# A three-layer CIN kernel on one core: set-up reordered, two weight rows made inside the loop, issue order fixed on all engines

## The chip, the cores and the metric

The kernel runs on one core of one Trainium2 chip. The metric is the device time of one execution in microseconds (us), the median over several executions. All times below are microseconds unless another unit is written. The span of a profile is from the first to the last instruction. The execution profiled before the change took 556.77 (span 555.0), more than the median of 552.89.

The engines are TensorE (PE, with its weight loads as PEld), VectorE (DVE), ScalarE (ACT), GpSimd (POOL) and SyncE (SP), which only starts DMAs here. TensorE has a granted clock, recorded in the profile: 1.00 is full speed, 0.50 is half.

## The reference

The input is x of shape (1024, 64, 16): batch, fields, embedding. Three layers multiply fields pairwise and contract the products with a weight:

```python
def _cin_forward(x, Ws, bs, fc_w, fc_b, split_half=True):
    x0 = x
    h = x
    xs = []
    n = len(Ws)                       # 3 layers of 128 channels
    for i in range(n):
        z = jnp.einsum('bfe,bge->bfge', x0, h)
        ...
        y = jnp.einsum('oc,bce->boe', Ws[i], z) + bs[i][None, :, None]
        if split_half and i != n - 1:
            half = y.shape[1] // 2
            x_i, h = (y[:, :half, :], y[:, half:, :])
        else:
            x_i, h = (y, y)
        xs.append(x_i)
    pooled = jnp.sum(jnp.concatenate(xs, axis=1), axis=2)
    return pooled @ fc_w.T + fc_b
```

The result is one number per batch row, and everything behind the second product is linear. Both kernels therefore fold `fc_w` into the weights first (set-up: a vector V2 from W2, a matrix M from V2 and W1, rows V1 and V0 from the other halves of W1 and W0), and then need, per chunk of 32 batch rows, only the pairwise products of x and one contraction of 17 matmuls.

## The kernel before

There are 32 chunks. Each has four products `z` made by VectorE (2.29 each), each of which feeds four matmuls, then a matmul of squares. Every second chunk closes a pair: TensorE makes one more matmul, `y`, VectorE multiplies it into `uu` and reduces. These are the parts that matter:

```python
    xp = ctx.enter_context(tc.tile_pool(name="xp", bufs=3))
    zp = ctx.enter_context(tc.tile_pool(name="zp", bufs=3))
    ...
    pv2 = ps.tile([128, 32], F32, tag="set", name="pv2", bufs=4)      # V2: 32 matmuls of one column
    for k in range(32):
        nc.tensor.matmul(pv2[:, k : k + 1], w2s[:, k, :], fc2, start=True, stop=True)
    ...
    for k in range(4):                                                # V1 and V0, in set-up
        w01 = setup.tile([128, 1024], F32, tag="w01", name=f"w01_{k}")
        nc.sync.dma_start(out=w01, in_=wv01[:, k * 1024 : (k + 1) * 1024])
        for m in range(2):
            pv = ps.tile([2, 512], F32, tag="set", name=f"pv_{k}_{m}", bufs=4)
            nc.tensor.matmul(pv, fc01, w01[:, m * 512 : (m + 1) * 512], start=True, stop=True)
            ...
    def products(c, j):
        z = zp.tile([128, NI, N], F32, tag="z", name="z")
        nc.vector.tensor_tensor(
            z, xas[c], xbs[c][:, j, :].unsqueeze(1).to_broadcast([128, NI, N]), ALU.mult
        )
        for i in range(NI):
            t = j * NI + i
            nc.tensor.matmul(accs[c], w_all[:, t, :], z[:, i, :], start=(t == 0), stop=False)
    ...
    def combine(c):
        ...
        nc.scalar.copy(q, accs[c][64:128])
        nc.vector.scalar_tensor_tensor(uu[to, 0, :], accs[c][0:64], bh1, q, ALU.add, ALU.mult)
        if half == 0:
            return
        y = ps.tile([128, N], F32, tag="y", name=f"y_{c}", bufs=1)
        nc.tensor.matmul(y, bd, xxs[c // 2], start=True, stop=True)
        nc.vector.scalar_tensor_tensor(uu[:, 1, :], y, cx, xxs[c // 2], ALU.add, ALU.mult)
        nc.vector.tensor_reduce(
            acc[:, :, c // 2, :], uu.rearrange("p k (b e) -> p k b e", e=E), AX.X, ALU.add
        )

    for c in range(NCH + 1):
        if c + 1 < NCH:
            load_chunk(c + 1)
        if c < NCH:
            accs[c] = ps.tile([128, N], F32, tag="acc", name=f"acc_{c}")
            products(c, 0)
            products(c, 1)
        if c > 0:
            combine(c - 1)
        if c < NCH:
            products(c, 2)
            products(c, 3)
            squares(c)
```

The text puts `combine` in the middle of a chunk, but before the change this text was not the issue order: the scheduler of the language was free to put instructions that don't depend on one another in another order on each engine, and did.

Of the kernel before, what the change touches and what calls it, by code (L numbers as in the profile page):

```python
# [26 lines left out]
F32 = mybir.dt.float32  # L27
AF = mybir.ActivationFunctionType
ALU = mybir.AluOpType
AX = mybir.AxisListType  # L30

F = 64
# [12 lines left out]
def cin_kernel(ctx, tc, x2, w0a, w0b, w1h, wv2, wv01, b0, b1, b2, fc_w, fc_b, out):  # L45
    nc = tc.nc
    const = ctx.enter_context(tc.tile_pool(name="const", bufs=1))
    setup = ctx.enter_context(tc.tile_pool(name="setup", bufs=2))
    xp = ctx.enter_context(tc.tile_pool(name="xp", bufs=3))
    zp = ctx.enter_context(tc.tile_pool(name="zp", bufs=3))  # L50
    sp = ctx.enter_context(tc.tile_pool(name="sp", bufs=2))
    ps = ctx.enter_context(tc.tile_pool(name="ps", bufs=2, space=bass.MemoryType.PSUM))
# [9 lines left out]


    fc01 = const.tile([128, 2], F32, tag="fc01", name="fc01")
    fc2 = const.tile([128, 1], F32, tag="fc2", name="fc2")
    nc.gpsimd.memset(fc01, 0.0)
    nc.scalar.dma_start(out=fc2, in_=fc_w[0, 128:256].unsqueeze(1))
    nc.scalar.dma_start(out=fc01[0:64, 0:1], in_=fc_w[0, 0:64].unsqueeze(1))
    nc.scalar.dma_start(out=fc01[64:128, 1:2], in_=fc_w[0, 64:128].unsqueeze(1))
    bh1 = const.tile([F, 1], F32, tag="bh1", name="bh1")  # L70
# [6 lines left out]
    nc.gpsimd.dma_start(out=bh1, in_=b0c[64:128])  # L77
# [20 lines left out]


    w2s = const.tile([128, 32, 128], F32, tag="w2s", name="w2s")  # L100
    w1s = const.tile([128, 32 * F], F32, tag="w1s", name="w1s")
    w0t = const.tile([128, NT + 1, F], F32, tag="w0t", name="w0t")
    w0u = const.tile([128, NT, F], F32, tag="w0u", name="w0u")
    for k in range(4):
        nc.sync.dma_start(out=w2s[:, 8 * k : 8 * k + 8, :], in_=wv2[:, 8 * k : 8 * k + 8, :])
    nc.sync.dma_start(out=w1s, in_=w1h)

    xas, xbs, zls, xxs = {}, {}, {}, {}

    def load_chunk(c):  # L110
        xa = xp.tile([128, NI, N], F32, tag="xa", name=f"xa_{c}")
        xb = xp.tile([128, NJ, N], F32, tag="xb", name=f"xb_{c}")
        zl = xp.tile([128, N], F32, tag="zl", name=f"zl_{c}")
        for half in range(2):
            to = slice(half * F, (half + 1) * F)
            nc.sync.dma_start(out=xa[to], in_=rows(c, 0, [[1, NI]]))
            nc.sync.dma_start(out=xb[to], in_=rows(c, 16 * half + 4, [[4, NJ]]))
        nc.sync.dma_start(out=zl[F:128], in_=rows(c, 0, []))
        if c % 2 == 0:
            xxs[c // 2] = sp.tile([128, N], F32, tag="xx", name=f"xx_{c}")  # L120
        to = slice(c % 2 * F, (c % 2 + 1) * F)
        nc.sync.dma_start(out=xxs[c // 2][to], in_=rows(c, 0, []))
        xas[c], xbs[c], zls[c] = xa, xb, zl

    load_chunk(0)
# [5 lines left out]
    pv2 = ps.tile([128, 32], F32, tag="set", name="pv2", bufs=4)  # L131
    for k in range(32):
        nc.tensor.matmul(pv2[:, k : k + 1], w2s[:, k, :], fc2, start=True, stop=True)  # L133
    for half in range(2):
        to = slice(half * F, (half + 1) * F)
        nc.vector.tensor_copy(v2t[to, 0:32], pv2[0:64])  # L136
        nc.vector.tensor_copy(v2t[to, 32:64], pv2[64:128])  # L137
# [3 lines left out]
    m_sb = const.tile([F, F, F], F32, tag="m_sb", name="m_sb")  # L141
    for m in range(4):
        for half in range(2):
            to = slice(half * F, (half + 1) * F)
            pm = ps.tile([F, 512], F32, tag="set", name=f"pm_{m}_{half}", bufs=4)
            nc.tensor.matmul(  # L146
                pm, v2t[to], w1s[to, m * 512 : (m + 1) * 512], start=True, stop=True
            )
            f0 = half * 32 + m * 8
            m_to = m_sb[:, f0 : f0 + 8, :].rearrange("p f g -> p (f g)")  # L150
            if half:
                nc.vector.tensor_copy(m_to, pm)  # L152
            else:
                nc.scalar.copy(m_to, pm)
    md = dr.tile([EXT, EXT, F], F32, tag="md", name="md")
    nc.scalar.dma_start(out=md[0:64, 0:64, :], in_=m_sb)
    nc.scalar.dma_start(out=md[64:96, 0:64, :], in_=m_sb[0:32])
    nc.scalar.dma_start(out=md[0:64, 64:96, :], in_=m_sb[:, 0:32, :])
    nc.scalar.dma_start(out=md[64:96, 64:68, :], in_=m_sb[0:32, 0:4, :])
    nc.scalar.dma_start(out=md[64:68, 64:96, :], in_=m_sb[0:4, 0:32, :])  # L160
# [9 lines left out]
    for half in range(2):  # L170
        to = slice(half * F, (half + 1) * F)
        b = 16 * half + 4
        nc.scalar.dma_start(
            out=ms1[to].rearrange("p (j i) g -> p j (i g)", i=NI),
            in_=skewed(b * row, [[4 * row, NJ], [1, NI * F]]),
        )
        for i in range(NI):
            nc.scalar.dma_start(
                out=ms2[to].rearrange("p (j i) g -> p j i g", i=NI)[:, :, i, :],
                in_=skewed(i * row + b * F, [[4 * F, NJ], [1, F]]),  # L180
            )
    nc.scalar.dma_start(out=w_all[0:64, NT, 64:128], in_=skewed(0, [[1, F]]))

    nc.vector.memset(ms2[64:128, 3 * NI, :], 0.0)  # L184
    nc.vector.memset(w0u[64:128, 3 * NI, :], 0.0)
    nc.vector.tensor_tensor(w_all[:, 0:NT, 0:64], w0t[:, 0:NT, :], w0u, ALU.add)
    nc.vector.tensor_copy(w_all[0:64, NT, 0:64], w0t[0:64, NT, :])
    nc.vector.tensor_tensor(w_all[:, 0:NT, 64:128], ms1, ms2, ALU.add)  # L188


    vrow = const.tile([2, F * F], F32, tag="vrow", name="vrow")
    for k in range(4):
        w01 = setup.tile([128, 1024], F32, tag="w01", name=f"w01_{k}")
        nc.sync.dma_start(out=w01, in_=wv01[:, k * 1024 : (k + 1) * 1024])
        for m in range(2):
            pv = ps.tile([2, 512], F32, tag="set", name=f"pv_{k}_{m}", bufs=4)
            nc.tensor.matmul(pv, fc01, w01[:, m * 512 : (m + 1) * 512], start=True, stop=True)  # L197
            col = (2 * k + m) * 512
            nc.scalar.copy(vrow[:, col : col + 512], pv)  # L199
    nc.scalar.dma_start(  # L200
        out=w_all[64:128, NT, 64:128], in_=vrow[1:2, :].rearrange("o (f g) -> o f g", g=F)
    )
    for half in range(2):
        to = slice(half * F, (half + 1) * F)
        nc.scalar.dma_start(
            out=bd[to, to], in_=vrow[0:1, :].rearrange("o (f g) -> o f g", g=F)
        )


    cx = const.tile([128, 1], F32, tag="cx", name="cx")  # L210
    pcx = ps.tile([128, 1], F32, tag="set", name="pcx", bufs=4)
    for half in range(2):
        nc.tensor.matmul(
            pcx[half * F : (half + 1) * F], v2t[0:64], bh2, start=True, stop=True
        )
    nc.scalar.copy(cx, pcx)
    cst = const.tile([1, 1], F32, tag="cst", name="cst")
    pc = ps.tile([1, 1], F32, tag="set", name="pc", bufs=4)
    for j in range(2):
        nc.tensor.matmul(  # L220
            pc, fcol[:, j : j + 1], bcol[:, j : j + 1], start=(j == 0), stop=(j == 1)
        )
    nc.scalar.activation(cst, pc, AF.Identity, bias=fcb, scale=float(E))
# [5 lines left out]
    def products(c, j):  # L229
        z = zp.tile([128, NI, N], F32, tag="z", name="z")  # L230
        nc.vector.tensor_tensor(  # L231
            z, xas[c], xbs[c][:, j, :].unsqueeze(1).to_broadcast([128, NI, N]), ALU.mult
        )
        for i in range(NI):
            t = j * NI + i
            nc.tensor.matmul(accs[c], w_all[:, t, :], z[:, i, :], start=(t == 0), stop=False)  # L236

    def squares(c):
        nc.scalar.activation(zls[c][0:64], xas[c][0:64, 0, :], AF.Square)  # L239
        nc.tensor.matmul(accs[c], w_all[:, NT, :], zls[c], start=False, stop=True)  # L240

    def combine(c):
        half = c % 2
        to = slice(half * F, (half + 1) * F)
        if half == 0:
            uus[c // 2] = sp.tile([128, 2, N], F32, tag="uu", name=f"uu_{c}")
        uu = uus[c // 2]
        q = sp.tile([F, N], F32, tag="q", name=f"q_{c}")
        nc.scalar.copy(q, accs[c][64:128])  # L249
        nc.vector.scalar_tensor_tensor(uu[to, 0, :], accs[c][0:64], bh1, q, ALU.add, ALU.mult)  # L250
        if half == 0:
            return
        y = ps.tile([128, N], F32, tag="y", name=f"y_{c}", bufs=1)
        nc.tensor.matmul(y, bd, xxs[c // 2], start=True, stop=True)  # L254
        nc.vector.scalar_tensor_tensor(uu[:, 1, :], y, cx, xxs[c // 2], ALU.add, ALU.mult)  # L255
        nc.vector.tensor_reduce(  # L256
            acc[:, :, c // 2, :], uu.rearrange("p k (b e) -> p k b e", e=E), AX.X, ALU.add
        )

    for c in range(NCH + 1):  # L260
        if c + 1 < NCH:
            load_chunk(c + 1)
        if c < NCH:
            accs[c] = ps.tile([128, N], F32, tag="acc", name=f"acc_{c}")
            products(c, 0)
            products(c, 1)
        if c > 0:
            combine(c - 1)
# [7 lines left out]
    for k in range(2):  # L276
        po = ps.tile([1, 2, half_pairs * CB], F32, tag="set", name=f"po_{k}", bufs=4)
# [63 lines left out]
```

## Time and profile before

| | before |
|---|---|
| median of 3 runs | 552.89 (551.77 to 554.76) |
| profiled span, mean granted clock | 555.0, 0.975 |
| first product matmul | 66.3 |
| TensorE busy, share of the span | 515.9, 93% |
| one pair of chunks in the loop | 30.04 |

Most lines that show this are in the prediction below. Two more matter. They are groups of the page: line, engine, operation, output and inputs with their sizes and the count; then busy time and the mean ns of one; then the engine's idle time just before them and what ended most of it.

```profile
L236 PE MATMUL acc<-z,w_all 128*128 128x512 f32 x1024 | 447.2, 592 | 0.0
L231 DVE TENSOR_TENSOR z<-xa,xb 128x2048 f32<-128x2048 f32 x128 | 293.3, 2292 | 135.9 <-PE acc L236 134.6
```

TensorE never idles in front of a product pass (0.0). VectorE idles 135.9 in front of its products, and 134.6 of that ends when TensorE frees a buffer. VectorE is ahead, and TensorE sets the pace.

### The profile page before, as it was taken

How to read it: one execution, taken by the hardware profiler on the slowest of the kernel's cores; microseconds unless marked ns; L12 is line 12 of the kernel's file. 1: busy time of each engine (PE TensorE's matmuls, PEld its weight loads, DVE VectorE, ACT ScalarE, POOL GpSimd, SP SyncE). 2: the span in 40 equal slices, each digit the busy share in tenths (PEclk: the TensorE clock that was granted, in tenths of full speed). 3: DMA queues.
4: the chain of work that ended last, by engine and by line, in shares of the span. 5: the costliest groups of instructions: out<-in, count | busy, mean ns of one | idle time of the engine just before them, and what ended most of it. 6: DMA issues, size and time to landing. Idle time of an engine off the chain costs nothing.

```text
span 555.0 us, 3402 instructions
## 1 busy us (share of the span) xinstructions
PE 515.9 (93%) x1240; PEld 231.9 (42%) x1240; DVE 352.0 (63%) x205; ACT 44.9 (8%) x81; POOL 5.3 (1%) x18
## 2 busy tenths in 40 slices
PE   5803799999999999999999999999999999999997
PEld 5600144444444444444444444444444444444442
DVE  0250076768677677768676867767776867686751
ACT  0100300000000000000000000000000000000001
POOL 3000000000000000000000000000000000000000
PEclk9967699999999999999999999999999999999999
DMA  8999998787777777877778777777787877874000
GB/s 254 185 283 210 205 208 170 144 163 146 156 153 159 150 152 162 180 161 161 160 147 165 146 154 154 154 150 154 161 180 161 165 155 151 162 152 77 0 1 0
DMA packets 33114, 85.33 MB, mean 154 GB/s; under 512 B 6405, under 2 KB 6949, under 8 KB 28710
## 3 DMA queue, kind: packets, MB, share of 16 engines
q1 hardware_dynamic: 29234, 81.84, 71.1%
q10 hardware_dynamic: 3608, 3.28, 2.8%
q8 instruction: 10, 0.16, 0.2%
q14 instruction: 6, 0.05, 0.0%
q0 software_dynamic: 256, 0.00, 0.0%
HBM read 82.89 MB, written 2.17 MB: 153 GB/s over the span
## 4 chain that ended last, share of the span: by engine, by line
PE 92%; DMA 6%; DVE 0%; ACT 0%; issue 0%; ACTq 0%; SPq 0%
PE acc L236 79%; PE acc L240 5%; DMA w<-in_wv 3%; PE pv L133 2%; PE y L254 2%; PE pv L197 2%; DMA ms<-md 1%; DMA fc<-in_fc_w 1%; DMA md<-m_sb 1%; PE pm L146 1%; PE po L281 0%; DVE acc L256 0%; DVE uu L255 0%; ACT res L289 0%; ACT q L249 0%
## 5 line engine op out<-in xcount | busy, mean ns | idle before, releaser
L236 PE MATMUL acc<-z,w_all 128*128 128x512 f32 x1024 | 447.2, 592 | 0.0
L231 DVE TENSOR_TENSOR z<-xa,xb 128x2048 f32<-128x2048 f32 x128 | 293.3, 2292 | 135.9 <-PE acc L236 134.6
L236 PEld LDWEIGHTS acc<-z,w_all 128*128 128x128 f32 x1024 | 194.5, 190 | 244.5 <-issue 244.4
L249 ACT COPY q<-acc 64x512 f32<-64x512 f32 x32 | 18.6, 582 | 443.8 <-PE acc L240 443.8
L197 PE MATMUL pv<-w,fc 128*2 128x512 f32 x16 | 11.5, 887 | 27.9 <-DMA w<-in_wv 14.9
L240 PE MATMUL acc<-zl,w_all 128*128 128x512 f32 x64 | 32.7, 592 | 0.0
L250 DVE SCALAR_TENSOR_TENSOR uu<-acc,bh,q 64x512 f32<-64x512 f32 x32 | 23.7, 740 | 10.0 <-ACT q L249 9.5
L239 ACT ACTIVATE zl<-xa 64x512 f32<-64x512 f32 x32 | 20.1, 628 | 3.6 <-DMA xa<-in_x 3.6
L133 PE MATMUL pv<-fc,w2s 128*128 128x1 f32 x64 | 13.8, 352 | 6.6 <-DMA fc<-in_fc_w 6.6
L256 DVE TENSOR_REDUCE acc<-uu 128x64 f32<-128x1024 f32 x16 | 19.5, 1220 | 0.5
L240 PEld LDWEIGHTS acc<-zl,w_all 128*128 128x128 f32 x64 | 12.2, 190 | 15.3 <-issue 15.3
L197 PEld LDWEIGHTS pv<-w,fc 128*2 128x2 f32 x16 | 1.6, 108 | 37.6 <-issue 21.5
L133 PEld LDWEIGHTS pv<-fc,w2s 128*128 128x128 f32 x64 | 13.7, 332 | 6.6 <-DMA fc<-in_fc_w 6.6
L254 PE MATMUL y<-xx,bd 128*128 128x512 f32 x32 | 16.3, 592 | 0.0
L136 DVE COPY v2t<-pv 64x32 f32<-64x32 f32 x2 | 0.4, 184 | 20.4 <-PE pv L133 20.4
L255 DVE SCALAR_TENSOR_TENSOR uu<-y,cx,xx 128x512 f32<-128x512 f32 x16 | 11.9, 745 | 0.0
L188 DVE TENSOR_TENSOR w_all<-ms,ms 128x1024 f32<-128x1024 f32 x1 | 1.2, 1224 | 13.2 <-DMA ms<-md 13.2
L254 PEld LDWEIGHTS y<-xx,bd 128*128 128x128 f32 x32 | 6.1, 190 | 7.7 <-issue 7.7
L199 ACT COPY vrow<-pv 2x512 f32<-2x512 f32 x8 | 4.2, 570 | 33.3 <-DMA ms<-md 32.2
L184 DVE MEMSET ms<- 64x64 f32 x1 | 0.1, 112 | 9.7 <-DMA ms<-md 9.7
L146 PE MATMUL pm<-w1s,v2t 64*64 64x512 f32 x16 | 5.6, 809 | 0.5 <-DVE v2t L137 0.5
L152 DVE COPY m_sb<-pm 64x512 f32<-64x512 f32 x4 | 2.7, 683 | 3.2 <-PE pm L146 3.2
(33 smaller groups left out, 21.0 us busy)
## 6 DMA issues: line engine op xcount, KB each, us to landing
xa<-in_x SPq DMA_DIRECT2D x64, 512.0 KB, 5.8
xb<-in_x SPq DMA_DIRECT2D x64, 512.0 KB, 7.1
zl<-in_x SPq DMA_DIRECT2D x32, 128.0 KB, 4.2
xx<-in_x SPq DMA_DIRECT2D x32, 128.0 KB, 4.1
w2s<-in_wv SPq DMA_DIRECT2D x4, 512.0 KB, 7.8
w<-in_wv SPq DMA_DIRECT2D x4, 512.0 KB, 11.9
w1s<-in_w1h SPq DMA_DIRECT2D x1, 1024.0 KB, 13.4
md<-m_sb ACTq DMA_DIRECT2D x2, 512.0 KB, 7.1
```

The costliest lines, as they stand in the source:

```text
L133: nc.tensor.matmul(pv2[:, k : k + 1], w2s[:, k, :], fc2, start=True, stop=True)
L146: nc.tensor.matmul(pm, v2t[to], w1s[to, m * 512 : (m + 1) * 512], start=True, stop=True)
L197: nc.tensor.matmul(pv, fc01, w01[:, m * 512 : (m + 1) * 512], start=True, stop=True)
L231: nc.vector.tensor_tensor(z, xas[c], xbs[c][:, j, :].unsqueeze(1).to_broadcast([128, NI, N]), ALU.mult)
L236: nc.tensor.matmul(accs[c], w_all[:, t, :], z[:, i, :], start=(t == 0), stop=False)
L239: nc.scalar.activation(zls[c][0:64], xas[c][0:64, 0, :], AF.Square)
L240: nc.tensor.matmul(accs[c], w_all[:, NT, :], zls[c], start=False, stop=True)
L249: nc.scalar.copy(q, accs[c][64:128])
L250: nc.vector.scalar_tensor_tensor(uu[to, 0, :], accs[c][0:64], bh1, q, ALU.add, ALU.mult)
L254: nc.tensor.matmul(y, bd, xxs[c // 2], start=True, stop=True)
L255: nc.vector.scalar_tensor_tensor(uu[:, 1, :], y, cx, xxs[c // 2], ALU.add, ALU.mult)
L256: nc.vector.tensor_reduce(acc[:, :, c // 2, :], uu.rearrange("p k (b e) -> p k b e", e=E), AX.X, ALU.add)
```

## The change

The intent is a shorter set-up. W2 becomes the moving operand, so V2 takes 8 wide matmuls instead of 32 of one column. Transfers have one fixed order, with the rows for V1 and V0 (2 MB) taken out of set-up into the loop. And the order in which the program text issues work is made binding on every engine, by one line near the top. The core of the diff, cuts marked with dots:

```diff
     nc = tc.nc
+    ctx.enter_context(tc.manual_schedule())
     const = ctx.enter_context(tc.tile_pool(name="const", bufs=1))
-    setup = ctx.enter_context(tc.tile_pool(name="setup", bufs=2))
-    zp = ctx.enter_context(tc.tile_pool(name="zp", bufs=3))
+    zp = ctx.enter_context(tc.tile_pool(name="zp", bufs=7))
...
-    for k in range(32):
-        nc.tensor.matmul(pv2[:, k : k + 1], w2s[:, k, :], fc2, start=True, stop=True)
+    for k in range(2):
+        vrow = big(f"v2row_{k}")
+        for m in range(4):
+            pv = ps.tile([1, 512], F32, tag="set", name=f"pv2_{k}_{m}")
+            nc.tensor.matmul(pv, fc2, w2s[k][:, cols], start=True, stop=True)
+            ...
+        for half in range(2):
+            nc.scalar.dma_start(out=v2t[half * F + k * 32 : half * F + (k + 1) * 32], ...)
...
+    def v_row(name, fc, wx, outs):
+        w = big(f"w_{name}")
+        nc.sync.dma_start(out=w, in_=wx)
+        ...  # 8 matmuls of 64 rows x 512, ScalarE copies, row sent by DMA
...
+    def sums(k):
+        y = ps.tile([128, N], F32, tag="y", name=f"y_{k}", bufs=1)
+        nc.tensor.matmul(y, bd, xxs[k], start=True, stop=True)
+        nc.vector.scalar_tensor_tensor(uus[k][:, 1, :], y, cx, xxs[k], ALU.add, ALU.mult)
         nc.vector.tensor_reduce(
...
+    for j in range(NJ):
+        contract(0, j, zs[j])
+    v_row("v1", fc1, wx1, [w_all[64:128, NT, 64:128]])
+    constants()
+    load_chunk(2)
+    for c in range(1, NCH + 1):
+        if c + 2 < NCH:
+            load_chunk(c + 2)
         if c < NCH:
+            new_acc(c)
             products(c, 0)
             products(c, 1)
+        if c == 1:
+            nc.tensor.matmul(accs[0], w_all[:, NT, :], zls[0], start=False, stop=True)
+        factors(c - 1)
+        if c == 2:
+            v_row("v0", fc0, wx0, [bd[to, to] for to in halves])
+        if c % 2 == 0:
+            sums(c // 2 - 1)
         if c < NCH:
             products(c, 2)
             products(c, 3)
             squares(c)
```

## The prediction

Its sum came to 659 of span (657 of time), and terms in it are cut: 0.7 of the 5.6 of chunk 1 (1.2 + 3.7 + 0.7), 4 of clock losses in the 18 of chunk 2 (4 + 5.5 + 4.6 + 4), and the reasoning by which the clock falls in about 4 of the 14 gaps, which was not shown; the 10 that followed from it still stands in the sum. The two rounds of reads were an estimate, and so are the 2.5 for a cold start: in the trace before, the passes from 41.41 and from 59.61 came 0.85 apart until the clock rose at 44.7 and 65.1, and half of these 3.3 and 5.5 is 1.7 and 2.8. A window is 3.41, here and below.

> **What bounds the kernel now.** I read three views, in this order: the busy time by stretches, the chain that ended last in order of time, and VectorE's instructions of one steady stretch. All times below are microseconds unless ns is written. The stretches (columns: length, then busy time and count of TensorE matmul, weight load, VectorE, ScalarE, GpSimd, then granted clock, DMA share, GB/s):
>
> ```profile
> 20.40:26.60 6.20, 5.63 (x16) 2.30 (x16) 2.89 (x8) 2.56 (x5) 0.00 (x0) 1.00 1.01 204
> 26.60:41.40 14.80, 0.00 (x0) 0.02 (x1) 8.64 (x7) 0.17 (x1) 0.00 (x0) 0.65 0.94 266
> 41.40:66.30 24.90, 11.89 (x25) 1.97 (x25) 1.34 (x2) 3.68 (x7) 0.00 (x0) 0.66 1.02 204
> 66.30:546.30 480.00, 480.00 (x1120) 212.62 (x1120) 336.38 (x186) 35.22 (x65) 0.00 (x0) 1.00 0.72 146
> 546.30:555.00 8.70, 4.59 (x19) 1.23 (x17) 2.71 (x3) 1.94 (x3) 0.00 (x0) 1.00 0.00 0
> ```
>
> Set-up lasts until 66.3, with DMA saturated and TensorE mostly idle. From there to 546.3 TensorE issues 1120 matmul passes without one gap (480.0 / 1120 = 0.429 each; an fp32 matmul is two passes). 8.7 of tail follow. The loop in the chain (start, length, what):
>
> ```profile
> 66.32 13.93 PE acc L236 x32
> 80.25 0.86 PE acc L240 x2
> 81.11 13.73 PE acc L236 x32
> 94.84 0.86 PE acc L240 x2
> 95.70 6.87 PE acc L236 x16
> 102.57 0.86 PE y L254 x2
> 103.42 6.87 PE acc L236 x16
> ```
>
> A chunk is 16 product matmuls (13.73) and one of squares (0.86); every second chunk has a y in its middle. A pair costs 30.04, all TensorE. So the loop can only get longer, and the whole prize is in the 66.3 of set-up. The loop is free of gaps because VectorE runs ahead:
>
> ```profile
> 252.81 2.29 DVE L231 TENSOR_TENSOR z<-xa,xb 128x2048 f32<-128x2048 f32 x1 [1.14 <-PE acc L236]
> 255.02 0.74 DVE L255 SCALAR_TENSOR_TENSOR uu<-y,cx,xx 128x512 f32<-128x512 f32 x1
> 255.80 1.22 DVE L256 TENSOR_REDUCE acc<-uu 128x64 f32<-128x1024 f32 x1
> 257.10 2.29 DVE L231 TENSOR_TENSOR z<-xa,xb 128x2048 f32<-128x2048 f32 x1
> ```
>
> The y of this pair came from TensorE at 252.8 (chain); VectorE first made another z and took y at 255.0, 2.2 after. The wait in front of a z is for TensorE to free a buffer: VectorE is three products ahead, and y's work fits into its slack.
>
> [...] what carries my prediction is that the built program's order on each engine is the order of execution. [...] the clock fell at 31.0 after matmuls ended at 26.5, rose at 44.7 (matmuls from 41.4), fell at 51.5, rose at 65.1 (from 59.6). These times lie 13.6, 6.8 and 13.6 apart[...]. [...]
>
> **The change, part by part.**
>
> *V2.* Before, 64 passes of one column took 13.8 (6.6 to 20.4) and gave V2 in columns, ready at 20.8. After, 8 matmuls of 512 columns are 16 passes of 0.43 = 6.9, from the first landing of W2 (issue 0.8 + 6.8 = 7.6) to about 14.6. But V2 is now a row in one partition: copy 0.6, two DMA issues 1.0, and 6.6 to land (bd<-vrow, the same kind of transfer, 6.4 to 6.7) make 22.8. V2 comes 2 later, not earlier.
>
> *Table md.* TensorE then idled for 8, so the 16 passes of M (5.6 before) start at half clock, about 8.0: end 30.8. Seven writes follow; the seventh overlaps the sixth in a corner of md and waits until it has landed. 2.06 MB at 266 GB/s (rate of 26.6 to 41.4) are 7.7, so about 39; the seventh needs at least 4.2 (shortest md write): 43. The first read started at 38.6 before: 4.5 later.
>
> *Reads of md.* Before, 38.6 to 63.0 = 24.4[...]. After, half are issued on SyncE, ahead of chunk 1. Two rounds remain[...]: 6 + 6.5 (reads took 5.1 to 10.2), then 0.11 + 1.22 for zero and sum: 43 + 12.5 + 1.3 = about 57. VectorE is not later: the mirrored half by ScalarE at 39.5 + 4 x 0.58 = 41.8, then 4 x 2.29 + 2.9 = 53.9. I take the first product matmul at 56, 10 earlier than 66.3.
>
> *Moved into the loop.* V1 and V0 are 16 matmuls x 2 x 0.43 = 13.7, and two small constants 0.4. These were inside the 66.3 before, and now stand in the stream that sets the end. The stream also starts cold now: 2.5[...].
>
> *Chunk 1.* The squares matmul of chunk 0 waits for V1's DMA: copy 0.6 + issues 1.1 + landing 6.8 = 8.5 against 0.4 + 6.9 of matmuls, 1.2 of idle. Then, in VectorE's order, z(1,2) stands behind factors(0), which waits for that matmul: 0.6 (q) + 0.75 + 2.29 = 3.7. [...]
>
> *Chunk 2.* wx0 (1 MB) is issued after chunk 4's loads, which wait for VectorE and for TensorE's squares of chunk 1; it lands about 4 too late. y stands right behind V0 and needs V0's row: 0.6 + 4 issues + landing = 5.5. Then 4.6 as in the next part[...]: 18.
>
> *Fixed issue order, the step that decides.* In the order of the built program, VectorE has in each even chunk z(c,0), z(c,1), factors, uu(y), reduce, z(c,2). TensorE has the matmuls of z(c,1), y, those of z(c,2). So y, uu, reduce, z(c,2), matmul are a serial chain: y's last pass ends 0.16 after its slot (592 - 429 ns), then 0.78 to reduce, 1.30 to z, 2.29 for z (pitches in the lines above), and 0.1 of signals: 4.6 of TensorE idle. Seven z buffers don't help, as z(c,2) is behind uu in a FIFO. Odd chunks lose nothing: q 0.6, uu 0.75, z 2.29 fit beside 6.87 of matmuls. Chunks 4 to 30, 14 of them: 14 x 4.6 = 64.4. [...] about 4 cold restarts of 2.5, 10.
>
> *Sum.* 56 + 488.7 (66.3 to 555.0 as before) + 2.5 + 14.1 + 5.6 + 18 + 64.4 + 10 = 659 of span; the median time lies 2.1 below the span: 657.
>
> **The rivals.** (1) The set-up gain carries, and the loop stays gapless: 552.9 - 10 + 14 + 2.5, about 559; with set-up down to 45, about 548. For it: less traffic ahead of the loop (2 MB of rows, 0.5 of mirror, chunk 1) in a stretch where DMA is at 1.02. Against: it needs VectorE to get past uu(y), which the order forbids. (2) Every gap halves the clock, because a mostly idle window also counts: 15 restarts of 2.5 instead of 4, about 685. The trace has only long idles, so it can't exclude this. (3) DMA becomes the bound: a pair needs 4.5 MB; at 200 GB/s that is 22.5, below 34.6; it can only matter around chunk 2, some 5 either way. (4) The reads of md stay slow (24 as before): first product at 69, about 670.
>
> **Range and chances.** Of the sum, 64 rests on durations that hardly vary and an order that I read; the clock (0 to 30), chunk 2 (10 to 25) and set-up (50 to 62) are loose. This gives 640 to 688. For "faster", the chain of y must be absent: 0.02; "same" 0.03; "slower" 0.95.
>
> **What would show it.** Right: TensorE idle of about 4.4 in front of the third product group of each even chunk, released by VectorE's z, VectorE's uu waiting for y; a pair of about 34.6 instead of 30.04; clock dips after some gaps only; first product at 50 to 62; V2 landed near 23; one idle of about 5 in front of y of chunk 2. Wrong: uu(y) taken without TensorE waiting, a pair of 30 to 31, or the first product before 45.

## The result, and the profile after

| | before | after |
|---|---|---|
| median of 4 runs | 553.03 (551.77 to 554.76) | 688.42 (686.68 to 691.01) |
| profiled span, mean granted clock | 555.0, 0.975 | 684.9, 0.890 |
| first product matmul | 66.3 | 59.4 |
| TensorE busy, share of the span | 515.9, 93% | 562.8, 82% |
| one pair in the steady loop | 30.04 | 37.55 |

The kernel became slower by a ratio of 1.2449, with a 95% interval of 1.2397 to 1.2501. A ratio here is the mean time of one kernel's fast runs over that of the other's of the same rounds, so it is not quite the ratio of the medians.

The same groups of the page, and that of `uu` made from y:

```profile
L248 PE MATMUL acc<-z,w_all 128*128 128x512 f32 x1024 | 495.2, 643 | 99.7 <-DVE z L240 68.1
L240 DVE TENSOR_TENSOR z<-xa,xb 128x2048 f32<-128x2048 f32 x128 | 284.4, 2280 | 16.0 <-ACT xa L178 14.5
...
L275 DVE SCALAR_TENSOR_TENSOR uu<-y,cx,xx 128x512 f32<-128x512 f32 x16 | 12.0, 751 | 108.1 <-PE y L274 108.0
```

The roles are exchanged. TensorE now idles 99.7 in front of its product passes, and 68.1 of that is ended by a `z` of VectorE. VectorE hardly waits in front of `z` any more (16.0, most of it in set-up); it waits 108.0 for `y` in front of `uu`. Besides, the mean pass went from 592 to 643 ns, with no change to the instruction: that is the clock, as an experiment below shows. Set-up, chunks 0 to 3, the 14 pairs of chunks 4 to 31, and the tail, in stretches (columns as in the prediction: length, busy of PE, PEld, DVE, ACT, POOL, granted clock, DMA share, GB/s). Up to the first clock record (11.8 here, 24.2 before the change) the view counts full speed, although the passes for V2 come 0.85 apart up to 11.9 and 0.43 after it; so the clock of set-up is lower than it says:

```profile
0.00:59.44 59.44, 15.32 (x32) 3.69 (x33) 17.11 (x17) 8.43 (x11) 7.75 (x22) 0.71 0.81 195
59.44:151.65 92.21, 78.21 (x179) 30.33 (x180) 35.10 (x19) 12.39 (x24) 0.00 (x0) 0.89 0.66 145
151.65:676.53 524.88, 464.72 (x981) 200.01 (x981) 290.52 (x166) 31.17 (x56) 0.00 (x0) 0.91 0.57 114
676.53:684.90 8.37, 4.55 (x18) 1.19 (x17) 2.71 (x3) 1.94 (x3) 0.00 (x0) 0.96 0.00 0
```

Set-up did shrink, by 6.9. The 14 pairs took 524.88, where 14 x 30.04 = 420.6 would be TensorE's work alone: 104.3 too much. TensorE idles 524.88 - 464.72 = 60.2 of it, 4.3 per pair; the other 44.1 went into busy time, at a mean clock of 0.91. The chain that ended last, in order of time (start, length, what), shows set-up and two of these pairs:

```profile
16.75 5.65 DMA v2t<-v2row
...
22.49 5.13 PE pm L164 x15
...
40.52 2.36 DMA md<-m
42.90 4.17 DMA ms<-md
...
59.44 15.77 PE acc L248 x32
...
195.67 0.87 PE y L274 x2
...
196.57 0.76 DVE uu L275
...
198.49 2.29 DVE z L240
...
200.82 9.88 PE acc L248 x16
...
613.44 10.07 PE acc L248 x16
```

In the pair at 195.67 the chain leaves TensorE after `y`, passes through VectorE (`uu`, the reduce, `z`), and comes back at 200.82. The 16 passes behind the gap then take 9.88, where 6.87 is their time at full speed. Late in the loop it is 10.07. VectorE's instructions of the same pair, with the wait in brackets:

```profile
196.57 0.75 DVE L275 SCALAR_TENSOR_TENSOR uu<-y,cx,xx 128x512 f32<-128x512 f32 x1 [6.37 <-PE y L274]
197.35 1.22 DVE L276 TENSOR_REDUCE acc<-uu 128x64 f32<-128x1024 f32 x1
198.49 8.89 DVE L240 TENSOR_TENSOR z<-xa,xb 128x2048 f32<-128x2048 f32 x4
```

VectorE stood still for 6.37 with seven buffers for `z` at hand, because `uu` was next in its order. Then it made four `z` without a pause. Finally the stretches between the clock's changes around this gap. The granted clock, the first of the last three figures, is read from the clock records:

```profile
196.15:199.56 3.41, 0.38 (x1) 0.00 (x0) 2.96 (x3) 0.00 (x0) 0.00 (x0) 1.00 0.00 0
199.56:202.97 3.41, 2.15 (x3) 1.11 (x4) 3.41 (x3) 0.00 (x0) 0.00 (x0) 0.50 0.00 0
202.97:206.38 3.41, 3.41 (x5) 1.33 (x5) 3.41 (x3) 0.00 (x0) 0.00 (x0) 0.50 0.61 159
206.38:237.10 30.72, 27.50 (x64) 11.84 (x63) 14.44 (x10) 2.23 (x4) 0.00 (x0) 1.00 0.69 136
```

TensorE was busy for 0.38 of the 3.41 in the window before the fall, so this window was not wholly idle (later in the loop it is, see below). The clock stayed at half for two windows: the rest of the gap, and 5.6 of work.

### The profile page after: what moved, and what is told of

Same layout as the page of the kernel before. It is cut to its first block, busy times and chain, and to the rows that moved or that the text cites. A ratio compares the mean times of both kernels' runs of the same rounds, so it can differ in the third digit from the quotient of the medians.

```text
span 684.9 us, 3299 instructions
## 1 busy us (share of the span) xinstructions
PE 562.8 (82%) x1208; PEld 235.2 (34%) x1208; DVE 345.5 (50%) x205; ACT 53.9 (8%) x94; POOL 7.8 (1%) x22
## 4 chain that ended last, share of the span: by engine, by line
PE 81%; DVE 8%; DMA 6%; issue 3%; ACTq 1%; ACT 1%; SPq 0%; DVEq 0%
PE acc L248 71%; DVE z L240 5%; PE acc L258 4%; PE y L274 2%; DVE uu L275 2%; DMA xa<-in_x 1%; PE pv L144 1%; PE pv_v L222 1%; DMA md<-m 1%; DMA w_v<-in_wx 1%; DMA v2t<-v2row 1%; DMA fc<-in_fc_w 1%; PE pm L164 1%; DMA ms<-md 1%; ACTq L173 0%
## 5 line engine op out<-in xcount | busy, mean ns | idle before, releaser
L248 PE MATMUL acc<-z,w_all 128*128 128x512 f32 x1024 | 495.2, 643 | 99.7 <-DVE z L240 68.1
L248 PEld LDWEIGHTS acc<-z,w_all 128*128 128x128 f32 x1024 | 210.0, 207 | 380.0 <-issue 258.4
L240 DVE TENSOR_TENSOR z<-xa,xb 128x2048 f32<-128x2048 f32 x128 | 284.4, 2280 | 16.0 <-ACT xa L178 14.5
L275 DVE SCALAR_TENSOR_TENSOR uu<-y,cx,xx 128x512 f32<-128x512 f32 x16 | 12.0, 751 | 108.1 <-PE y L274 108.0
L258 PEld LDWEIGHTS acc<-zl,w_all 128*128 128x128 f32 x62 | 11.8, 190 | 14.8 <-issue 14.8
L144 PE MATMUL pv<-w,fc 128*1 128x512 f32 x16 | 10.0, 790 | 5.9 <-DMA fc<-in_fc_w 5.9
L222 PE MATMUL pv_v<-w_v,fc 64*1 64x512 f32 x32 | 10.6, 588 | 1.7 <-DMA w_v<-in_wx 1.7
L223 ACT COPY vrow_v<-pv_v 1x512 f32<-1x512 f32 x16 | 8.6, 572 | 43.4 <-DMA xx<-in_x 32.6
L274 PEld LDWEIGHTS y<-xx,bd 128*128 128x128 f32 x32 | 6.2, 198 | 12.4 <-issue 12.4
L146 DVE COPY v2row<-pv 1x512 f32<-1x512 f32 x4 | 2.7, 678 | 14.0 <-PE pv L144 14.0
L166 DVE COPY m<-pm 64x512 f32<-64x512 f32 x4 | 2.7, 683 | 9.1 <-PE pm L164 9.1
L164 PEld LDWEIGHTS pm<-w1s,v2t 64*64 64x64 f32 x16 | 2.2, 180 | 9.7 <-issue 8.5
L335 PE MATMUL po<-acc,ones 128*1 128x256 f32 x16 | 3.8, 378 | 0.8 <-DVE acc L276 0.8
```

What stands on the lines that cost most here:

```text
L144: nc.tensor.matmul(pv, fc2, w2s[k][:, cols], start=True, stop=True)
L164: nc.tensor.matmul(pm, v2t[to], w1s[to, cols], start=True, stop=True)
L222: nc.tensor.matmul(pv, fc[halves[half]], w[halves[half], cols], start=True, stop=True)
L240: nc.vector.tensor_tensor(z, xas[c], xbs[c][:, j, :].unsqueeze(1).to_broadcast([128, NI, N]), ALU.mult)
L258: nc.tensor.matmul(accs[c], w_all[:, NT, :], zls[c], start=False, stop=True)
L274: nc.tensor.matmul(y, bd, xxs[k], start=True, stop=True)
```

## The experiments

The theory, formed from these lines: two things cost the loop time, and both come from where `y` stands in a fixed order. The first is the chain y, `uu`, reduce, `z`, matmul. The second is a clock that falls after nearly every gap. The rival for the second part was that something else slows the passes behind the gap, for instance a `z` that comes late. For the clock's rule itself, two readings were open: a wholly idle window is needed (the phase of the windows then happens to fit in every pair), or a mostly idle one is enough. A third question is which line of the change is to blame: the fixed order or the new set-up. All nine runs gave correct results.

### y first in the chunk: e1_y_first

The `y` of each even chunk from chunk 4 on is issued at the start of the chunk on TensorE. VectorE's order is not touched.

```diff
+    def linear(k):
+        ys[k] = ps.tile([128, N], F32, tag="y", name=f"y_{k}", bufs=1)
+        nc.tensor.matmul(ys[k], bd, xxs[k], start=True, stop=True)
...
+        if c % 2 == 0 and c > 2:
+            linear(c // 2 - 1)
         if c < NCH:
             new_acc(c)
             products(c, 0)
```

Expected:

> Only the y matmul of pairs 1 to 14 moves, from behind the second product group of the even chunk to before its first; VectorE's order is untouched. Theory A (the serial chain y, uu, reduce, z, matmul makes the gap, and the gap makes the clock fall): each of the 14 pairs of chunks 4 to 31 goes from about 37.5 to 30.04 us, 14 x 7.45 = 104 us less, so about 584 us, no TensorE gap in those chunks and a clock of 1.00 there. Rival B (the gaps come from elsewhere: the x loads, the deeper product buffers, the reduce itself): stays within 10 us of 688.

Measured: 586.02 (584.77 to 587.51), ratio to before 1.0585 (1.0556 to 1.0614). The stretch from 142.16 to the end of the loop:

```profile
142.16:572.00 429.84, 429.84 (x1003) 190.22 (x1002) 300.04 (x171) 32.28 (x58) 0.00 (x0) 1.00 0.72 145
```

TensorE is busy for all of it, at full clock. One moved matmul took 102 off the 688.4. So the gaps and the clock of the 14 pairs, 104.3 together in the trace, hang on the place of `y` on TensorE, given VectorE's fixed order. That VectorE's order stayed as it was shows that its fixed order is harmless as long as `y` is done early.

### Needless matmuls inside the gap: e2_fill_gap, e4_fill_1, e4_fill_3

If the clock is a cost of its own, then filling the gap with matmuls whose result is thrown away must make the kernel faster, although the chain through VectorE stays. Four, one or three matmuls follow `y`, which is how e2_fill_gap, e4_fill_1 and e4_fill_3 differ. One is two passes, 0.86.

```diff
         nc.tensor.matmul(y, bd, xxs[k], start=True, stop=True)
+        if 0 < k < NCH // 2 - 1:
+            idle_matmuls(4)
...
+    def idle_matmuls(n):
+        for _ in range(n):
+            pj = ps.tile([128, N], F32, tag="set", name="pj")
+            four = w_all[:, 0:NI, :].rearrange("p a b -> p (a b)")
+            nc.tensor.matmul(pj, w_all[:, 0, :], four, start=True, stop=True)
```

Expected of four:

> Four needless matmuls (4 x 0.86 = 3.43 us) stand on TensorE directly behind y in chunks 4 to 30, inside the gap of 4.3 us; the chain through VectorE is unchanged. Theory A: the gap costs 4.3 as before, but the clock no longer falls, so a pair is 34.3 us instead of 37.5: 688 - 14 x 3.15 = about 644 us. Rival D (the slow products after the gap are slow for another reason[...]): stays at 688, as the added work lies inside the gap.

Measured: 650.96, ratio to before 1.1762 (1.1736 to 1.1787), where 644 was expected. TensorE's groups around one gap of this run:

```profile
508.88 1.02 PE L274 MATMUL y<-xx,bd 128*128 128x512 f32 x2
509.74 3.60 PE L287 MATMUL pj<-w_all 128*128 128x512 f32 x8
514.21 7.13 PE L248 MATMUL acc<-z,w_all 128*128 128x512 f32 x16 [0.87 <-DVE z L240]
```

With four needless matmuls per pair, the kernel is 37.5 faster than without. The group behind the gap takes 7.13 instead of 10.07: the `z` comes no earlier (514.21 - 509.74 = 4.5 after `y` here, 4.3 there), but the clock is whole. So the rival "a late z slows the group" is out, and so is the recorded rival (688). The clock's share is 37.5, or a little more, as the gap is 0.2 longer here. The 7.13 against 6.87 also shows a restart cost of 0.26 that has nothing to do with the clock (0.16 of it is the last pass running on behind its slot, 592 - 429 ns).

Expected of one, which leaves an idle of 3.44 split over two windows of the clock:

> One needless matmul (0.86 us) directly behind y instead of four: TensorE's idle per gap shrinks from 4.3 to about 3.43 us, the chain through VectorE stays. Theory T (read off the clock records of the first four runs: the clock falls after a window of 3.413 us in which TensorE was busy for less than about 0.42 of it, so some 2.0 us of idle within one window are enough): it still falls in most pairs, about 680 us (674 to 688). Theory F (my prediction's: only a wholly idle window counts): an idle of 3.43 hardly ever holds one, so it never falls, about 651 us as with four.

Measured: 689.74 (683.72 to 692.91), ratio 1.2503 (1.2474 to 1.2532). This lies above the 674 to 688 of theory T, so less was gained than it said: nothing. In the profiled execution (686.05) the clock fell in 13 of the 14 pairs. One of them in the chain:

```profile
457.42 0.87 PE y L274 x2
...
460.24 2.29 DVE z L240
...
462.57 10.08 PE acc L248 x16
```

The group is as slow as in the changed kernel (10.08). By the clock records, TensorE was busy for 0.25 to 0.36 of the window before each of the 13 falls, so the reading that needs a wholly idle window is out.

Expected of three:

> Three needless matmuls: idle per gap about 1.71 us. Theory T: less than the 2.0 us needed in a window, so the clock never falls: about 651 us. Theory F: 651 too. Should it lie near 670 to 680, the threshold is below what the records showed.

Measured: 649.04 (median of the three fast runs, 647.03 to 651.87), ratio 1.1737 (1.1691 to 1.1782), as with four. By this time, an idle of about 1.7 (the expectation's estimate) did not bring the clock down. The profiled execution of this run was disturbed: it took 1560.5, with passes of 1432 ns in the mean instead of 592, and yet the view prints a granted clock of 1.000 for it. The statement about 1.7 rests on the time alone.

### Needless matmuls outside the gap: e3_plus_1, e3_plus_4

These two ask how the clock's windows and the pairs lie against each other. One or four needless matmuls stand behind the squares of each odd chunk from chunk 3 on, far from the gap.

```diff
             squares(c)
+            if c % 2 and c > 2:
+                idle_matmuls(1)
```

Expected of one:

> One needless matmul (0.86 us) is ADDED to TensorE's stream behind the squares of each odd chunk from chunk 3 on, outside the gap. Theory A with phase lock (the clock's windows of 3.413 us: 34.3 us of a pair lie 0.2 us over 10 windows, so after one fall the next gap always meets the same phase and the clock falls in every pair; 0.86 us more breaks this): cost 14 x 0.86 = 12, gain about 44 - 10 = 34 us, so about 667 us (662 to 671), FASTER than the kernel with less work, clock falling in about 3 or 4 of 14 pairs. Rival C (every gap of over 3.4 us makes the clock fall): 688 + 12 = 700 us.

Measured: 692.17, ratio 1.2506 (1.2477 to 1.2535). This missed: neither the 667 of "wholly idle window, phase by chance" nor the 700 of "every gap alike". Groups behind two successive gaps in its chain:

```profile
469.79 9.49 PE acc L248 x16
...
507.61 8.83 PE acc L248 x16
```

The group now varies from pair to pair, between 8.83 and 9.57, and never reaches 10.07. So the clock still fell after each gap, but 15 x 0.86 = 13 of added work made the kernel only 3.8 longer. (The expectations count 14 matmuls; the edit adds one behind each odd chunk from 3 to 31, and the trace has 30 passes, 15 matmuls.) The rest was given back, because the half-speed stretches ended earlier in the group (of the two above, the mean clock was 0.81 from 463 to 481 and 0.90 from 501 to 518). The pattern repeats after five pairs: the clock fell at 204.93, 392.66 and 580.39, 187.73 apart, which is 55 windows and the same 37.55 a pair as without the added work.

Expected of four:

> The same with four needless matmuls per pair (3.43 us, about one window). Theory A with phase lock: the pair is again 0.2 us over a whole number of windows, so it locks again: 12 windows = 40.96 us a pair, clock falling in every pair; 14 x 3.43 = 48 us more than the kernel, about 736 us, or some 10 to 18 less if it locks only after some pairs. An unlocked clock (as with one matmul, about 10 us of loss) would give about 702. Rival C: 736.

Measured: 741.25, ratio 1.3392 (1.3365 to 1.3418). The added work is 15 x 3.43 = 51.5, and the kernel is 52.8 longer than the 688.4: all of the work shows, and none is given back. A pair now takes 40.96, 12 windows of 3.4133, where it took 11 windows in the changed kernel (37.55). Both readings had said 736 here, so this run does not decide between them; why pairs settle on whole numbers of windows is taken up in the part on the prediction.

### Which line of the change: e5_free_order, e6_before_fixed

e5_free_order is the changed kernel without the one line, and e6_before_fixed is the kernel before with this line and nothing else of the change.

```diff
-    ctx.enter_context(tc.manual_schedule())
```

Expected:

> The changed kernel with the fixed issue order taken out (its one line), so that the scheduler orders the engines again; everything else of the change stays. Theory A (the fixed order alone makes the slowdown): VectorE runs ahead again, a pair costs 30.04 us and the clock stays up; the V rows in the loop add about 8 to 11 us and the new set-up takes about as much off or a little more: about 570 us (558 to 582). Rival G (the moved parts themselves, V rows in the loop and the deeper loads, cost most of the 135 us): over 620 us.

Measured: 567.53, ratio 1.0250 (1.0221 to 1.0279). Its loop in two stretches, as far as chunk 3 and behind it:

```profile
60.44:123.79 63.35, 59.17 (x137) 23.26 (x138) 29.93 (x16) 9.22 (x18) 0.00 (x0) 0.91 0.71 153
123.79:558.90 435.11, 435.11 (x1015) 192.59 (x1015) 299.28 (x168) 31.24 (x56) 0.00 (x0) 1.00 0.65 140
```

With the scheduler free, the loop behind 123.79 has no gap. `y` stands at the same place in TensorE's order as in the changed kernel (from the second pair on), behind the second product group of the even chunk, and it stood there before the change too. What differs is VectorE's order: counted in the traces, it makes three more `z` ahead of `uu` than the text has before the change, and six to eight more here. So the gap needs both, a `y` just in time on TensorE and a `uu` fixed in front of the next `z` on VectorE. (Moving `uu` back on VectorE, with the order still fixed, was not tried.)

The rest of the change is still a loss of 14, or 567.4 - 555.0 = 12.4 of span: the loop starts 5.9 earlier, but it idles 63.35 - 59.17 = 4.2, and TensorE is busy for 59.17 + 435.11 = 494.3 instead of 480.0. Of these 14.3, 9.3 are the V rows (24 of their 32 passes; 8 ran before the loop) and constants, and the other 5.0 go with the clock of 0.91.

Expected of the other direction:

> The kernel before with nothing but the fixed issue order added. Theory A: the same chain y, uu, reduce, z, matmul in program order, 15 pairs at about 37.5 instead of 30.04 us, and a later start of the loop (about 70 instead of 66 us, as VectorE's sums of the weights now stand in front of chunk 0's products): 553 + 15 x 7.45 + 4 to 10 = about 672 us (664 to 684). Rival G: the order is harmless with the old set-up, 553 to 570 us.

Measured: 669.63, ratio 1.2122 (1.2080 to 1.2163). One line added to the kernel before makes 116. Its chain shows the same links as the changed kernel:

```profile
252.87 0.87 PE y L255 x2
253.77 0.76 DVE uu L256
...
255.69 2.29 DVE z L232
...
258.02 10.06 PE acc L237 x16
```

The gap is 258.02 - 253.74 = 4.3, and the group behind it takes 10.06. So the fixed order alone, on the program text as it stood, makes 116, against 135 for the whole change; the new set-up isn't needed for it.

### Waits taken out of the fixed order: e7_repaired

The last kernel keeps the fixed order and repairs what it exposed. `y` is first in every even chunk; V1 and V0 are made in set-up, at a place where TensorE idles; the squares of chunk 0 stay in chunk 0; and the seventh write of the table no longer overlaps the sixth.

```diff
-    nc.scalar.dma_start(out=md[64:68, 64:96, :], in_=m_lo[0:4])
+    nc.scalar.dma_start(out=md[64:68, 68:96, :], in_=m_lo[0:4, 4:32, :])
...
+    v_load("v1", wx1)
+    v_load("v0", wx0)
...
     zs += [product(0, j) for j in range(1, NJ)]
+    v_row("v1", fc1, [w_all[64:128, NT, 64:128]])
+    v_row("v0", fc0, [bd[to, to] for to in halves])
     load_chunk(1)
     second_weights()
+    constants()
...
+    nc.tensor.matmul(accs[0], w_all[:, NT, :], zls[0], start=False, stop=True)
...
+        if c % 2 == 0:
+            linear(c // 2 - 1)
...
-        if c == 2:
-            v_row("v0", fc0, wx0, [bd[to, to] for to in halves])
```

In this version the row copies are VectorE's, the rows are sent on GpSimd's queue, and ScalarE's work on chunk 0 stands ahead of the copies of M.

> The fixed order kept, its waits taken out: y stands first in every even chunk; V1 and V0 are made in set-up again (their weights loaded behind w0u, copied by VectorE behind chunk 0's products, their rows sent on GpSimd's queue), so no V work and no wait for its rows is left in the loop; ScalarE mirrors chunk 0 before the copies of M; the seventh md write no longer overlaps the sixth. Theory A: the loop is gapless as before (480 us), the tail 8.5, the clock costs 2 to 2.5 at its start, and the first product comes at 53 to 58 us instead of 66.3: about 546 us (542 to 553), a little under the kernel before at 553. Rival: the 2 MB of V weights, loaded beside the writes of md, push the first product to 62 us or later: 554 to 562.

Measured in five rounds on another chip, with the kernel before beside it: 550.55 (547.61 to 551.50) against 553.78, ratio 0.9935 (0.9913 to 0.9957).

```profile
0.00:58.32 58.32, 32.13 (x72) 6.98 (x73) 27.20 (x33) 8.83 (x13) 10.72 (x28) 0.77 0.88 227
58.32:540.35 482.03, 482.03 (x1119) 213.38 (x1120) 325.62 (x185) 34.51 (x62) 0.00 (x0) 1.00 0.74 148
540.35:548.70 8.35, 4.66 (x19) 1.30 (x17) 2.71 (x3) 1.94 (x3) 0.00 (x0) 1.00 0.00 0
```

The loop is as tight as before (482.03, all busy, clock 1.00) and starts at 58.3 instead of 66.3. This is below both kernels: the changed one by 138, the one before by 3.2, or 0.65%. In the profiled executions the difference is 6.3 (548.7 against 555.0): 8.0 by the earlier start, less 2.0 that the loop is longer (482.0 against 480.0; its first 32 passes took 16.05, before the change 13.93). The timed runs differ by only half of this because the execution profiled before the change was a slower one: 556.77, 3.0 above the median of 553.78, while that of e7_repaired (550.8) is close to its own. The gain is clear of noise by its interval, but small.

## Why the prediction was right or wrong

The direction, the chain and the share of set-up were right. The time was just outside the range: 688.42 against 688 at its upper end. The terms of the sum, against the trace (span 684.9 against 659 predicted):

| term of the prediction | predicted | measured | difference |
|---|---|---|---|
| first product matmul at | 56 | 59.4 | +3.4 |
| cold start of the stream | 2.5 | 15.77 - 13.73 = 2.0 | -0.5 |
| V rows and constants | 14.1 | 10.9 | -3.2 |
| chunk 1 | 5.6 | 6.1 | +0.5 |
| chunk 2 | 18 | 13.9 | -4.1 |
| 14 gaps | 64.4 | 60.2 | -4.2 |
| clock of the 14 pairs | 10 | 44.1 | +34.1 |
| tail | 8.7 | 8.4 | -0.3 |

The differences add up to 25.7, of the 25.9 to explain. Two things belong to this table. The clock's 44.1 holds the restarts, 14 x 0.26 = 3.6, of which 2.2 (0.16 each) stood in the gaps of the prediction. And that the number came so near was luck: the other terms together were 8.4 too large and hid a quarter of what the clock was short. Taking 2.1 off the span for the time was wrong too, as the time is 1.8 longer than the span (686.68 against 684.9).

**The step that failed** is the one that ends in "about 4 cold restarts of 2.5, 10". Its reasoning, that only a wholly idle window brings the clock down and that chance decides whether a gap holds one, was not shown by any trace. There were 14 falls of the clock in 14 gaps, and they cost 44.1 / 14 = 3.15 each with the restart, not 2.5. Both halves of the step were wrong.

First, no whole window is needed. I added up TensorE's busy time in each window of 3.4133 of the grid that the clock records give, in the changed kernel and in the variants with needless matmuls. After a window with a busy share of 0.40 or less the clock fell (0.40 in e3_plus_1, 389.25 to 392.66); after one of 0.42 or more it stayed (0.42 in e3_plus_1, 314.15 to 317.57). Exceptions, falls at 0.59 to 0.64 (0.59 in the changed kernel, 114.23 to 117.64), were only in windows that held the passes for V0, whose weight has 64 rows and one column; in e5_free_order a window that such passes filled (54.35 to 57.76) even left the clock at half: eight of them took 6.98 from 51.32, 0.87 each, and the next 32 passes 16.04. Once at half, in the changed kernel, it rose only after a window of at least 0.88 (22.07 to 25.48); after 0.74 or less it stayed (612.57 to 615.98). So about 3.41 x 0.60 = 2.0 of idle within one window was enough in these runs, an estimate from the 0.40. In the changed kernel the windows before the falls were busy for 0.23, 0.11, 0.05, 0.03 and 0.01 of their length in the first five of the 14 pairs, and from the sixth on they were idle. So its late pairs do hold a whole idle window, and would fit the reading that needs one; its first pairs and e4_fill_1 (3.44 of idle, fell 13 of 14 times) do not. e4_fill_3 (1.7, by its time never) bounds the rule from the other side.

Second, the phase was no lottery. In the changed kernel the groups behind the gap took 9.68, 9.88, 9.98, 10.02, 10.05, 10.06 and 10.07 from one pair to the next, each half as far from 10.07 as the one before (in e6_before_fixed 9.74, 9.91, 9.99, 10.03 and 10.06). Each time the clock was at half for exactly two windows, and at full for exactly nine between. The reason I give for it is argued from these numbers, and fits the variants: a gap that ends later by d leaves d less time before the grid's next rise of the clock, so d/2 less is lost, and the next gap is late by only d/2. The pair settles where 30.04 of work + 4.3 of gap + 3.2 of slow group = 37.5, which is 11 x 3.4133 = 37.55. With four needless matmuls outside the gap it settles at 12 windows, 40.96. With one, five pairs together settle at 55 windows (groups of 9.55, 9.38, 8.83, 9.49 and 8.83, over and over), and most of the added work is given back. Of the 3.2, 0.26 is the restart (7.13 in e2_fill_gap), and 5.96 of work at half speed (613.44 to 619.40, where the clock rose) makes 3.0.

My second rival had said "about 685", with 15 restarts of 2.5. It named the mechanism, and its number came close. I gave it too little weight: I wrote that the trace before "has only long idles, so it can't exclude this", and yet set the range as if the clock could cost at most 30 of time.

**The step that decides the sign** was right. The chain y, `uu`, reduce, `z`, matmul stands in the trace as written, released by VectorE's `z`, with `uu` waiting for `y`; and e6_before_fixed shows that the fixed order brings it, e1_y_first that an earlier `y` takes it away. Its size was 4.3 instead of 4.6: reduce to `z` took 198.49 - 197.35 = 1.14 instead of 1.30, and the trace counts from the end of `y`, where I had counted from its slot, 0.16 earlier. One line was misread: 252.8 is when `y` of the pair shown began; it ended at 253.6, so VectorE took it 1.4 after, not 2.2. The slack it was to show is there all the same. Odd chunks lost nothing, as expected.

**Set-up.** V2 landed at 22.4 (22.8 expected). The matmuls of M ended at 27.8, not 30.8: the 16 passes took 5.3, not 8.0, at a mean clock of 0.72. I had taken 5.6 as their time at full speed, but before the change, too, they came 0.43 apart up to the first clock record at 24.2 and 0.21 after it; the 1.00 of that stretch only stands for a missing record. The seventh write landed at 42.9 (43), but the sum of the weights waited until 58.1 instead of 55.5: behind the first read the chain has 10.26 of a transfer of chunk 1 (`xa`) between 47.7 and 58.0, where I had put two rounds of reads, 12.5 together, behind 43. That is 2.6 of the 3.4 of later start; the other 0.8 is that my own terms add up to 56.8, and I took 56.

**V rows.** 16 passes of V1 took 5.24, 0.33 each, instead of 6.9. The estimate used the full pitch of 0.43. In the trace four pairs of these passes start within 0.01 of each other, so 16 passes took the time of 12; which rows each of them used, the trace does not say. V0 I set at the same 5.3, since only 12 of its passes lie in one piece of the chain.

**Chunks 1 and 2.** The squares of chunk 0 waited less than thought, and chunk 1's loss came from its gap (3.6) and a half-speed stretch (2.0). In chunk 2, W0's rows came 1.7 late instead of 4, and the wait in front of `y` was 4.3 instead of 5.5.

**Of the other rivals,** the gapless loop did not come (pair 37.55). DMA was not the bound: its share is 0.57 in the 14 pairs. The reads of the table were faster than the pessimistic case (first product at 59.4, not 69).

The loss by parts, then, from runs: fixed order on the old set-up +116 (e6_before_fixed); everything else of the change, with the order free, +14 (e5_free_order); of the 135 in all, 102 go with the place of `y` in 14 pairs (e1_y_first), and the 35 between e1_y_first and e7_repaired (which ends 3 below the kernel before) lie in chunks 0 to 2 and set-up, which e7_repaired changes together and which I did not separate.

## What to carry to other kernels

When an issue order becomes fixed, go through each engine's order for a wait that used to be overtaken: here a producer issued just in time on one engine (`y` on TensorE) turned into a gap of 4.3 on it, because the consumer (`uu`) was fixed, on the other engine, in front of what the first engine needed next (`z`). Issue a matmul whose result another engine needs well ahead of that point; here one moved matmul was worth 102. And count a gap on TensorE at more than its length: here a gap of 4.3 cost 7.5 (4.3 and 3.2 of slow group), and four needless matmuls per pair made the kernel 37.5 faster (e2_fill_gap).
